# A two-layer graph network on one core: loop relations loaded two groups ahead, a last block read with 128 partitions, a ring of 30 gathered rows

## The chip, the cores and the metric

The kernel runs on one core of one Trainium2 chip. The metric is the time on the device in microseconds (us). Traces come from one profiled execution; times of kernels come from several.

## The reference

Two layers of a relational graph network over 50,000 nodes of 128 numbers and 850,000 edges (source, destination, one of 16 relations), sorted by destination. Every node has an edge to itself, a "loop", among them. All is float32.

```python
def layer(h, src, dst, rel, basis, w_comp, loop_w, bias):
    W = einsum('rb,bio->rio', w_comp, basis)          # 16 relations from 8 bases
    agg = segment_sum(h[src], dst * 16 + rel)         # per node and relation
    return relu(einsum('nri,rio->no', agg, W) + h @ loop_w + bias)

h = layer(x, ...); h = layer(h, ...)
out = layernorm(x + h)
```

## The kernel before

The 800,000 edges that are not loops are packed into 12,500 *tiles* of 128 edges; ten tiles make a *chunk* `c` (625 in a layer), five a half chunk. For each tile a gather (`gather`, L184, an indirect DMA that POOL issues) fetches the 128 source rows into a place `g` of a ring; a matmul (L1112, in `pa`) multiplies the place by the one-hot weights `hot`, ACT copies the result to `aT` (L1126). Every four chunks are multiplied by the bases (L796), turned (L805), spread over the nodes' slots on DVE (L779) and added to the nodes' sums with matmuls of L840. The ring has `RING * PER` = 5 x 5 = 25 places; after the last matmul of a half chunk `fetch` issues the gathers of the five tiles that stand 25 further. So a gather waits for the matmul that last read its place. The first 25 gathers of a layer go out at once.

Of every 45 or 50 tiles one is not gathered by POOL: SP or ACT copies its 128 rows one by one (`row_by_row`, L1022), finishing four half chunks (`LEAD`) ahead of their use, into places outside the ring.

Nodes are handled in *groups* `g` of 512 (98 in a layer; group 97 is smaller). `own_of_all` makes each group's loop part beside the chunks, two steps a chunk. `from_itself` loads `h_own`, the rows of four groups (L710, on SP, 128 partitions of 8 KB; 53 partitions for groups 96 and 97), at the first of each four; `loop_weights` then loads `lrel`, the loops' relations of the same four groups (L670, also on SP, 8 rows of 2 KB), and a step later small matmuls (L681, in `po<-twos,lrel`) and DVE (L689, L633, L662) make weights of it. Two more steps on, the transposes of `h_own` (L726) and the matmuls of L746 follow. At a layer's end the last sums are made by L768.

The edges are sorted out while layer 1 runs, by `later_rows`: `runs` closes up 128 runs of 672 edges a time and writes the others to `FULL` (L389) and the loops' relations to `LREL` (L444), both by indirect DMAs of POOL (scatters). `rows_of(j)` reads a block of closed-up runs back from `FULL` (L458, on SP, in two parts, of 1,280 numbers a partition), and DVE adds the parts (L465). The blocks start at rows 0, 16, 120, 248 and so on; the eleventh and last starts at 1,144 and has 106 rows. `own_of_all` takes care that the runs which a load of `lrel` needs have been stored, and notes up to where `LREL` has been read (`loaded`).

The order of the work on each engine is the order in which the code is written out: each engine runs its instructions in that order.

Of the kernel before, what the change touches and what calls it, by code (L numbers as in the profile page):

```python
# [39 lines left out]
F32 = mybir.dt.float32  # L40
# [10 lines left out]
P = 128  # L51
# [5 lines left out]
RUN = 672  # L57
HALF = K // 2
LIVE = HALF * P
# [8 lines left out]
BANK = 512  # L68
WEIGHTS = AT * PER * 8
BITS_AT_ONCE = BANK - WEIGHTS  # L70
RING = 5
SPANS = (9, 10)
LEAD = 4
HELD = 3
# [4 lines left out]
NEAR = 128  # L79
# [11 lines left out]
def tile_rgcn_resnorm(  # L91
# [16 lines left out]
    N, D = x.shape  # L108
    NR, NB = w_comp1.shape
    E = edges.shape[1] // 3  # L110
    R, M = -(-E // RUN), E - N
    C = -(-M // (K * P))
    NG = -(-R // P)
    GN, NGR = J * P, -(-N // (J * P))
    T = P // NR // 2

    ROWS = list(range(0, 2 * C, P)) if 2 * C <= P else [0, FIRST, *range(P - 8, 2 * C, P)]
    NP = NG * P * LIVE
# [14 lines left out]
    FULL = dram.tile([2 * NP, 2], F32, name="FULL")  # L133
# [62 lines left out]
    def column(j, first, ap):  # L196
# [3 lines left out]

    rows = [consts.tile([P, D], F32, name=f"g{i}") for i in range(RING * PER)]
    came_of = [tc.alloc_semaphore(f"row{i}") for i in range(RING * PER)]
    filled_times = [0] * (RING * PER)
    src = consts.tile([P, 2 * C * HALF], U16, name="src")

    APART = ((nc.sync, mybir.EngineType.SP), (nc.scalar, mybir.EngineType.Activation))
    apart = [
        [consts.tile([P, D], F32, name=f"g{RING * PER + HELD * i + j}") for j in range(HELD)] for i in range(len(APART))
    ]
# [47 lines left out]
    def set_up(pool):  # L257

        for h in range(2):
            nc.gpsimd.iota(  # L260
                spread[h],
                pattern=[[1, S]],
                base=-h * HALF * WN,
                channel_multiplier=-WN,
                allow_small_or_imprecise_dtypes=True,
            )
            ahead = pool.tile([HALF, S], F32, name="ahead")
            nc.vector.tensor_scalar(ahead, spread[h], 0.0, None, op0=OP.is_ge)
            nc.vector.scalar_tensor_tensor(spread[h], spread[h], float(WN), ahead, op0=OP.is_lt, op1=OP.mult)
        nc.gpsimd.iota(twos, pattern=[[2, T]], base=0, channel_multiplier=-1, allow_small_or_imprecise_dtypes=True)  # L270
        fits = pool.tile([2 * T, T], F32, name="fits")
        nc.vector.tensor_scalar(fits, twos, 0.0, None, op0=OP.is_le)
        nc.vector.scalar_tensor_tensor(twos, twos, -1.0, fits, op0=OP.is_ge, op1=OP.mult)
        later = pool.tile([HALF, 1], F32, name="later")
        nc.vector.tensor_scalar(later, part[:HALF], float(HALF), None, op0=OP.add)
        po = ps_o.tile([P, BANK], F32, name="po")
        nc.tensor.matmul(po[:S, :1], spread[0], part[:HALF], start=True, stop=False)
        nc.tensor.matmul(po[:S, :1], spread[1], later, start=False, stop=True)
        nc.vector.scalar_tensor_tensor(within[:S], po[:S, :1], float(-WN), part[:S], op0=OP.mult, op1=OP.add)
        yield  # L280
        none = pool.tile([P, NL // P], F32, name="none")
        nc.vector.memset(none, 0.0)
        for h in range(2):
            nc.sync.dma_start(LREL[h * NL : (h + 1) * NL].rearrange("(p k) o -> p (k o)", p=P), none)
        yield
# [166 lines left out]
    def rows_of(j, pool):  # L452

        r0 = ROWS[j]
        m = (ROWS[j + 1] if j + 1 < len(ROWS) else 2 * C) - r0
        parts = [pool.tile([P, LIVE, 2], F32, name=name) for name in ("full", "parts")]
        for h in range(2):
            nc.sync.dma_start(  # L458
                parts[h][:m],
                FULL[h * NP + r0 * LIVE : h * NP + (r0 + m) * LIVE].rearrange("(p e) w -> p e w", e=LIVE),  # L460
            )
        if j:
            yield
# [142 lines left out]
    def chunked():  # L606
        with (
# [5 lines left out]
            def ks(c):  # L613
                return min(K, -(-M // P) - c * K)
# [6 lines left out]
            def first(g):  # L621
                return max(0, -(-(g * GN - NEAR) // (N // C)) - 1)
# [7 lines left out]
            def summed_over(kinds, k):  # L630

                terms = hp.tile([P, K, NB, NR], F32, name="terms", bufs=1)[:, :k]
                nc.vector.tensor_tensor(  # L633
                    terms,
                    kinds[:, :, None, :].to_broadcast([P, k, NB, NR]),
                    table[:, None, :, :].to_broadcast([P, k, NB, NR]),
                    op=OP.mult,
                )
                return terms
# [23 lines left out]
                    weighed_for[i] = to  # L663
                    yield

            def loop_weights(g, n):

                few = min(T, NGR - g)
                of_nodes = hp.tile([2 * T, GN], F32, name="lrel", bufs=1)
                nc.sync.dma_start(  # L670
                    of_nodes[: 2 * few],
                    bass.AP(
                        tensor=LREL.tensor,
                        offset=LREL.offset + g * GN,
                        ap=[[GN, few], [NL, 2], [1, GN]],
                    ),
                )
                yield
                which_rel = ps_o.tile([P, BANK], F32, name="po")[:, : few * J]
                for j in range(J):  # L680
                    nc.tensor.matmul(  # L681
                        which_rel.rearrange("p (t j) -> p j t", j=J)[:, j],
                        of_nodes[: 2 * few].rearrange("q (p j) -> q j p", j=J)[:, j],
                        twos[: 2 * few, :few],
                        start=True,
                        stop=True,
                    )
                both = hp.tile([P, T * J, NR], U8, name="both_kinds", bufs=1)
                nc.vector.tensor_tensor(  # L689
                    both[:, : few * J],  # L690
                    col[:, None, 1 : NR + 1].to_broadcast([P, few * J, NR]),
                    which_rel[:, :, None].to_broadcast([P, few * J, NR]),
                    op=OP.is_equal,
                )
                yield
                lw = hp.tile([P, T * J, NB], F32, name="lw")
                for k in range(0, few * J, K):
                    m = min(K, few * J - k)
                    terms = summed_over(both[:, k : k + m], m)
                    nc.vector.tensor_reduce(lw[:, k : k + m], terms, AX.X, OP.add)  # L700
                yield lw.rearrange("p (t j) b -> p j t b", t=T)
# [175 lines left out]
                for _ in steps:  # L877
                    pass

            loaded, stored = [0], [1]  # L880
            rest_of_set_up = set_up(pr)
            next(rest_of_set_up)
            first_runs = runs(0, pr, lambda: 0)
# [16 lines left out]
            def later_rows():  # L900
                g = 0
                for j in range(1, len(ROWS)):
                    while g < needed(j):
                        g += 1
                        yield from runs(g, pr, lambda: loaded[0])
                        stored[0] = g + 1
                    yield from rows_of(j, pr)
                    ready[0] = j
                while g < NG - 1:
                    g += 1  # L910
                    yield from runs(g, pr, lambda: loaded[0])
                    stored[0] = g + 1

            coming = later_rows()
            ordered = ExitStack()
            ordered.enter_context(tc.manual_schedule(engines={mybir.EngineType.PE, mybir.EngineType.Pool, mybir.EngineType.DVE, mybir.EngineType.Activation, mybir.EngineType.SP}))
            for n, of in enumerate((x, H1)):
# [31 lines left out]
                def own_of_all():  # L949

                    for g in range(NGR):
                        while now[0] < min(first(g) + LAG - 5, C - LAG - 2):
                            yield
                        if n == 0 and g % T == 0:
                            end = min(N, (g + T) * GN)
                            while stored[0] < min(NG, -(-(end + NEAR) * E // (N * RUN * P))):
                                next(coming)
                            loaded[0] = end
                        yield from from_itself(g, of, n)
                        made[0] = g + 1  # L960

                def add(c):

                    for g in to_nodes(c, n):
                        assert made[0] > g
                        ending.append(finish(g, n))
# [65 lines left out]
                def place_in_ring(t):  # L1032

                    turn, k = divmod(n * tiles + t, RING * PER)
                    return k if turn % 2 == 0 else k // PER * PER + PER - 1 - k % PER
# [39 lines left out]
                for c in range(C):  # L1075
# [6 lines left out]
                    if c == 0:  # L1082
                        fetch(range(RING * PER))
                        nc.vector.tensor_copy(table, COMP[n].rearrange("p r b -> p b r"))
# [18 lines left out]
                    for k in range(0, K, PER):  # L1103
                        m = min(PER, ks(c) - k)
# [47 lines left out]
    def summed():  # L1152
        L1 = dram.tile([N, D], F32, name="L1")
        L2 = dram.tile([N, D], F32, name="L2")
        with tc.tile_pool(name="io", bufs=2) as io, tc.tile_pool(name="sbf", bufs=2) as sb:
# [140 lines left out]
            nodes(L2, norm, also=x)  # L1296

    chunked()
    wrong = nc.values_load(bad[0:1, 0:1], min_val=0, max_val=1)
    with tc.If(wrong > 0):  # L1300
# [40 lines left out]
```

## Time and profile before

| | us |
|---|---|
| median of 3 runs (lowest, highest) | 15,246.5 (15,244.9, 15,247.5) |
| profiled execution, its own time | 15,244.2 |
| its span, first to last instruction | 15,242.5 |
| busy: PE, DVE, ACT, POOL | 11,634.5, 10,276.1, 2,167.7, 11,380.2 |
| first gather starts, first gather of layer 2 starts, end | 30.3, 7,665.0, 15,242.5 |

The granted clock of PE was 0.811 on average. In rows of the timeline, the first number is the start in us, the second how long it took; in brackets stands how long the engine had been idle, and what ended that. In rows of groups, "busy, mean ns | idle before" follow the count. "issue" is idle time in which nothing that the profile shows was waited for.

### The profile page before, as it was taken

Reading aid. Unit: us, or ns where it says so; the run is one execution under the profiler, and the core shown is the slowest. Engines: PE = TensorE matmul, PEld = TensorE weight load, DVE = VectorE, ACT = ScalarE, POOL = GpSimd, SP = SyncE. Lnnn points to the kernel's source line nnn. Section 1 sums busy time; section 2 is a strip of 40 time slices with the busy share of each in tenths; the row PEclk is TensorE's granted clock in tenths of the full one; section 3 lists DMA queues with packets and bytes.
Section 4 is the critical chain, followed back from the end, with each engine's and each line's share of the span. In section 5 each row is a group of like instructions: output and inputs, shape, how many; then the busy total and the mean of one; then the engine's idle time right before and its main releaser. Section 6 shows DMA issues by size and latency. Waiting matters only on the chain.

```text
span 15242.5 us, 256609 instructions
## 1 busy us (share of the span) xinstructions
PE 11634.5 (76%) x43954; PEld 7253.0 (48%) x43954; DVE 10276.1 (67%) x11737; ACT 2167.7 (14%) x4309; POOL 11380.2 (75%) x12013
## 2 busy tenths in 40 slices
PE   6777777777777777777777877777777777777777
PEld 4444444444444444444444444444444444444444
DVE  8777777777666666666666666666666666666666
ACT  1111111111111111111111111111111111111111
POOL 6777777777777777777777777777777777777776
PEclk8788888878888888888878888888788888878888
DMA  2333333323222222222222223222232223222322
GB/s 80 75 74 73 70 75 73 70 69 72 66 62 62 62 65 62 62 62 65 57 63 66 66 65 68 65 66 65 64 68 65 65 64 68 65 66 65 68 65 57
DMA packets 584455, 1013.83 MB, mean 67 GB/s; under 512 B 265788, under 2 KB 335420, under 8 KB 576543
## 3 DMA queue, kind: packets, MB, share of 16 engines
q0 software_dynamic: 385232, 792.77, 23.4%
q1 hardware_dynamic: 131496, 186.50, 4.4%
q10 hardware_dynamic: 66064, 18.03, 1.0%
q14 instruction: 1308, 10.71, 0.2%
q8 instruction: 355, 5.82, 0.2%
HBM read 924.65 MB, written 71.59 MB: 65 GB/s over the span
## 4 chain that ended last, share of the span: by engine, by line
POOL 15%; PE 15%; DMA 14%; issue 8%; ACTq 7%; SPq 4%; DVE 4%; ACT 1%; DVEq 0%; POOLq 0%
POOL g L184 15%; DMA g<-H,at 7%; PE po L796 6%; ACTq L1022 5%; DMA g<-in_x_dram,at 4%; SPq L1022 3%; PE pn L840 3%; PE pa L1112 3%; DMA lrel<-LREL 3%; ACTq L1015 2%; PE po L746 2%; DVE ls L761 1%; SPq L1015 1%; DVE terms L633 1%; DVE by L753 0%
## 5 line engine op out<-in xcount | busy, mean ns | idle before, releaser
L184 POOL DMA_INDIRECT g<-in_x_dram,at x5990 | 5689.7, 950 | 1907.9 <-issue 1701.5
L184 POOL DMA_INDIRECT g<-H,at x5990 | 5665.9, 946 | 1901.6 <-issue 1707.5
L1112 PEld LDWEIGHTS pa<-hot,g 128*128 128x128 f32 x25000 | 4250.8, 226 | 4305.6 <-issue 1628.6
L1112 PE MATMUL pa<-hot,g 128*128 128x96 f32 x25000 | 4799.7, 319 | 1914.1 <-DMA g<-H,at 953.0
L840 PE MATMUL pn<-slots,own 120*128 120x512 f32 x4128 | 2765.0, 797 | 701.0 <-DVE own L819 347.7
L753 DVE TENSOR_TENSOR by<-po,lw 128x512 f32<-128x512 f32 x1568 | 1074.2, 685 | 3207.3 <-PE po L746 3203.7
L1126 ACT COPY aT<-pa 128x480 f32<-128x480 f32 x2500 | 1395.5, 558 | 8454.8 <-PE pa L1112 3866.2
L796 PE MATMUL po<-aT,basis 128*128 128x480 f32 x4960 | 2335.8, 629 | 74.9 <-ACT aT L1126 74.5
L746 PE MATMUL po<-basis,hT 128*128 128x512 f32 x3136 | 1994.4, 723 | 387.3 <-ACT hT L732 320.4
L662 DVE TENSOR_REDUCE fixed<-terms 128x80 f32<-128x1280 f32 x1250 | 1864.1, 1491 | 30.4
L633 DVE TENSOR_TENSOR terms<-kinds,fixed 128x1280 f32<-128x1280 uint8 x1250 | 1848.6, 1479 | 12.2
L761 DVE TENSOR_REDUCE ls<-by 128x128 f32<-128x1152 f32 (+1 forms) x784 | 1659.1, 2116 | 33.7 <-DVE by L753 0.4
L796 PEld LDWEIGHTS po<-aT,basis 128*128 128x128 f32 x4960 | 1040.7, 216 | 1169.8 <-issue 1086.8
L840 PEld LDWEIGHTS pn<-slots,own 120*128 120x128 f32 x4128 | 898.8, 246 | 1340.2 <-issue 584.7
L929 DVE TENSOR_TENSOR hot<-fixed,own 128x960 f32<-128x960 f32 x1250 | 1438.7, 1151 | 40.5 <-PE pa L1112 18.6
L779 DVE TENSOR_TENSOR slots<-po,which 120x1024 f32<-120x1024 f32 (+1 forms) x630 | 759.9, 1206 | 197.0 <-PE po L805 167.3
L746 PEld LDWEIGHTS po<-basis,hT 128*128 128x128 f32 x3136 | 564.2, 225 | 424.7 <-ACT hT L732 346.7
L689 DVE TENSOR_TENSOR both_kinds<-col,po 128x256 uint8<-128x256 f32 (+1 forms) x50 | 20.8, 416 | 793.4 <-PE po L681 793.4
L819 DVE TENSOR_SCALAR own<-col,node 120x256 f32<-120x256 f32 (+1 forms) x1250 | 425.1, 341 | 7.5 <-PE pn L840 7.5
L800 ACT COPY by_slot<-po 128x480 f32<-128x480 f32 x310 | 173.3, 559 | 1778.2 <-PE po L796 1636.8
L681 PE MATMUL po<-twos,lrel 8*128 8x4 f32 (+1 forms) x400 | 100.4, 370 | 413.4 <-DMA lrel<-LREL 413.4
L1049 ACT CAST at<-src 128x20 int32<-128x20 uint16 x626 | 129.7, 207 | 1929.0 <-issue 1922.7
(143 smaller groups left out, 3957.3 us busy)
## 6 DMA issues: line engine op xcount, KB each, us to landing
g<-in_x_dram SPq DMA_DIRECT2D x17536, 0.5 KB
g<-H SPq DMA_DIRECT2D x17536, 0.5 KB
g<-in_x_dram ACTq DMA_DIRECT2D x15744, 0.5 KB
g<-H ACTq DMA_DIRECT2D x15744, 0.5 KB
g<-in_x_dram,at POOLq DMA_INDIRECT x5990
g<-H,at POOLq DMA_INDIRECT x5990
H<-ls SPq DMA_DIRECT2D x97, 256.0 KB
xw<-in_x_dram SPq DMA_DIRECT2D x97, 256.0 KB
```

The source lines that it names most:

```text
L184: return nc.gpsimd.indirect_dma_start(out=to, out_offset=None, in_=of, in_offset=bass.IndirectOffsetOnAxis(ap=idx, axis=0))
L633: nc.vector.tensor_tensor(terms, kinds[:, :, None, :].to_broadcast([P, k, NB, NR]), table[:, None, :, :].to_broadcast([P, k, NB, NR]), op= ...
L662: nc.vector.tensor_reduce(to[:, : ks(i)], terms, AX.X, OP.add)
L746: nc.tensor.matmul(hb[:m], hT[:, j, :m], BASIS[n][:, b : b + few, :].rearrange("p b d -> p (b d)"), start=True, stop=True,)
L753: nc.vector.tensor_tensor(by[:m, b : b + few, :], hb[:m].rearrange("p (b d) -> p b d", d=D), lw[:m, j, g % T, b : b + few, None].to_broadc ...
L761: nc.vector.tensor_reduce(ls[:m, j, :], by[:m].rearrange("p b d -> p d b"), AX.X, OP.add)
L796: nc.tensor.matmul(ps[:, : BATCH * S], BASIS[n][:, b, :], aT[:, b, :], start=b == 0, stop=b == NB - 1)
L840: nc.tensor.matmul(sums[g], own, of[:k].rearrange("s j d -> s (j d)"), start=c == first(g), stop=c == final(g),)
L929: nc.vector.tensor_tensor(hot[:, : ks(c)], pm[:, : ks(c), :, None].to_broadcast([P, ks(c), NB, WN]), own[:, : ks(c), None, :].to_broadcast ...
L1022: row = by.dma_start(to[e : e + 1, :].bitcast(U8), flat[ds(places[e % LOADED], 4 * D)].rearrange("(o d) -> o d", o=1),)
L1112: product = nc.tensor.matmul(pa[:, i * NB * WN : (i + 1) * NB * WN], row, hot[:, k + i].rearrange("e b w -> e (b w)"), start=True, stop=Tr ...
L1126: nc.scalar.copy(aT[:, :, place_of + k * WN : place_of + (k + m) * WN].rearrange("d b (i w) -> d i b w", w=WN), pa[:, : m * NB * WN].rearr ...
```

## The change

Three things: `RING` is 6, so the ring has 30 places and a half chunk's gathers stand 30 tiles ahead. `lrel` is loaded by a function of its own, `ask_loops`, called for the next four groups when the third of the present four begins, and for the second layer when the first has no group left. The last block of closed-up runs is read with 128 partitions, of which 106 are used.

```diff
-RING = 5
+RING = 6
...
+        read = P if j == len(ROWS) - 1 and r0 + P <= NG * P else m
         for h in range(2):
             nc.sync.dma_start(
-                parts[h][:m],
-                FULL[h * NP + r0 * LIVE : h * NP + (r0 + m) * LIVE].rearrange("(p e) w -> p e w", e=LIVE),
+                parts[h][:read],
+                FULL[h * NP + r0 * LIVE : h * NP + (r0 + read) * LIVE].rearrange("(p e) w -> p e w", e=LIVE),
             )
...
-            def loop_weights(g, n):
+            def ask_loops(g, n):
 
-                few = min(T, NGR - g)
-                of_nodes = hp.tile([2 * T, GN], F32, name="lrel", bufs=1)
+                end, few = min(N, (g + T) * GN), min(T, NGR - g)
+                if n == 0:
+                    while stored[0] < min(NG, -(-(end + NEAR) * E // (N * RUN * P))):
+                        next(coming)
+                    loaded[0] = end
+                asked[0] = hp.tile([2 * T, GN], F32, name="lrel", bufs=1)
                 nc.sync.dma_start(
-                    of_nodes[: 2 * few],
+                    asked[0][: 2 * few],
...
+            def loop_weights(g, n):
+
+                few = min(T, NGR - g)
+                of_nodes = asked[0]
                 yield
...
-                        if n == 0 and g % T == 0:
-                            end = min(N, (g + T) * GN)
-                            while stored[0] < min(NG, -(-(end + NEAR) * E // (N * RUN * P))):
-                                next(coming)
-                            loaded[0] = end
+                        if g == n == 0:
+                            ask_loops(g, n)
+                        elif g % T == T // 2 and g + T // 2 < NGR:
+                            ask_loops(g + T // 2, n)
                         yield from from_itself(g, of, n)
                         made[0] = g + 1
+                    if n == 0:
+                        ask_loops(0, 1)
```

Line numbers of the changed kernel are 1 to 11 higher. PE and DVE run the same instructions in the same order as before.

On POOL, at the start of layer 1, stand the gathers of the first tiles. The names g_86 to g_115 are the places of the ring; the next round begins with g_90, g_89 and so on. Before, from the 25th gather:

```order
L184 DMA g_110<-in_x_dram,at 128x128
L184 DMA g_90<-in_x_dram,at 128x128
L184 DMA g_89<-in_x_dram,at 128x128
L184 DMA g_88<-in_x_dram,at 128x128
L184 DMA g_87<-in_x_dram,at 128x128
L184 DMA g_86<-in_x_dram,at 128x128
L444 DMA LREL<-l_rel,l_to 100352x1
```

And now, from the same gather:

```order
L184 DMA g_110<-in_x_dram,at 128x128
L184 DMA g_111<-in_x_dram,at 128x128
L184 DMA g_112<-in_x_dram,at 128x128
L184 DMA g_113<-in_x_dram,at 128x128
L184 DMA g_114<-in_x_dram,at 128x128
L184 DMA g_115<-in_x_dram,at 128x128
L184 DMA g_90<-in_x_dram,at 128x128
L184 DMA g_89<-in_x_dram,at 128x128
L184 DMA g_88<-in_x_dram,at 128x128
L184 DMA g_87<-in_x_dram,at 128x128
L184 DMA g_86<-in_x_dram,at 128x128
L444 DMA LREL<-l_rel,l_to 100352x1
```

Five gathers have come in ahead of the first one that needs a place freed, and the scatter to LREL stands five gathers later.

On SP, near the end of layer 1, the loads for groups 96 and 97 stand among the copies of single rows (g_112, TENSOR_LOAD fetches their addresses). Before:

```order
L1015 TENSOR_LOAD far
L1022 DMA g_112<-in_x_dram 1x512 x8
L710 DMA h_own<-in_x_dram 53x2048
L670 DMA lrel<-LREL 4x1x512
L1022 DMA g_112<-in_x_dram 1x512 x24
```

Now the load of lrel, and 28 rows of the order later that of h_own:

```order
L1033 DMA g_117<-in_x_dram 1x512 x18
L675 DMA lrel<-LREL 4x1x512
L1033 DMA g_117<-in_x_dram 1x512 x14
L1026 TENSOR_LOAD far
L1033 DMA g_118<-in_x_dram 1x512 x32
```

```order
L1033 DMA g_117<-in_x_dram 1x512 x32
L1026 TENSOR_LOAD far
L1033 DMA g_117<-in_x_dram 1x512 x8
L720 DMA h_own<-in_x_dram 53x2048
L1033 DMA g_117<-in_x_dram 1x512 x24
```

lrel has moved ahead of the copies of several tiles; h_own stands where it stood, with nothing of lrel behind it.

More of the change, by code (lines that the diff above doesn't have):

```diff
@@ L878, in done @@
                     pass
-            loaded, stored = [0], [1]
+            loaded, stored, asked = [0], [1], [None]
             rest_of_set_up = set_up(pr)
```

## The prediction

> **What bounds the kernel now.** I read the page's engine line first, then its groups, then POOL in the timeline and in the waits by stretch. No engine is busy the whole time, and the chain of waits spreads over many lines, so neither names the bound. The two gather groups on POOL do.
>
> ```profile
> PE 11634.5 (76%) x43954; PEld 7253.0 (48%) x43954; DVE 10276.1 (67%) x11737; ACT 2167.7 (14%) x4309; POOL 11380.2 (75%) x12013
> POOL 15%; PE 15%; DMA 14%; issue 8%; ACTq 7%; SPq 4%; DVE 4%; ACT 1%; DVEq 0%; POOLq 0%
> L184 POOL DMA_INDIRECT g<-in_x_dram,at x5990 | 5689.7, 950 | 1907.9 <-issue 1701.5
> L184 POOL DMA_INDIRECT g<-H,at x5990 | 5665.9, 946 | 1901.6 <-issue 1707.5
> ...
> 3003.32 0.95 POOL L184 DMA_INDIRECT g<-in_x_dram,at  x1 [0.30 <-issue]
> 3004.57 0.94 POOL L184 DMA_INDIRECT g<-in_x_dram,at  x1 [0.31 <-issue]
> ```
>
> A gather takes 0.948 us (11,355.6 over 11,980) and the next starts 0.30 us after its end, waiting for nothing that is shown: one gather per 1.253 us. In 11,980 gathers that pace alone is 15,010 us of the 15,242.5, so POOL is the bound although the page calls it 75% busy. Whatever shortens another engine's wait helps only where POOL itself stood still. The idle time before gathers is 3,809.5 us; 11,980 gaps of 0.305 make 3,654, so 156 us are real stops. The waits of POOL in ten consecutive stretches say where. The rows are, in order, from 0:125 (two), 125:3900, 3900:4000, 4000:7500, 7500:7570, 7570:7660, 7660:7700, 7700:15060, 15060:15130 and 15130:15243; columns are total us, times, longest.
>
> ```profile
> POOL g L184 <- PE pa L1112: 9.5, 1, 9.5
> POOL g L184 <- ACT at L1049: 8.5, 1, 8.5
> POOL g L184 <- PE pa L1112: 53.0, 126, 5.4
> POOL g L184 <- PE pa L1112: 14.7, 4, 13.8
> POOL g L184 <- PE pa L1112: 43.6, 131, 3.2
> POOL g L184 <- PE pa L1112: 17.0, 3, 16.3
> POOL g L184 <- PE pa L1112: 13.4, 4, 6.1
> POOL g L184 <- DMA lrel<-LREL: 16.0, 1, 16.0
> POOL g L184 <- PE pa L1112: 107.1, 277, 5.3
> POOL g L184 <- PE pa L1112: 16.9, 2, 16.6
> POOL g L184 <- PE pa L1112: 14.4, 6, 8.3
> ```
>
> Less 0.305 for each time these are 9.2, 8.2, 14.6, 13.5, 3.6, 16.1, 12.2, 15.7, 22.6, 16.3 and 12.6 us. "PE pa L1112" means that the ring is full: the place that POOL wants is freed by a matmul of L1112, and PE was late. The 8.2 (first numbers of rows) and the 15.7 (the second layer gathers from H, which has to be complete) are not touched by the change.
>
> **Relations of loops.** Here is one group of four in the middle: the two loads on SP, the matmul that reads lrel, POOL's stop behind it, and the transposes that read h_own.
>
> ```profile
> 13838.09 0.37 SPq L710 DMA_DIRECT2D h_own<-H  x1
> 13838.50 0.68 SPq L670 DMA_DIRECT2D lrel<-LREL  x1
> 13854.84 2.02 PE L681 MATMUL po<-twos,lrel 8*128 8x4 f32 x8 [12.93 <-DMA lrel<-LREL]
> 13860.58 0.94 POOL L184 DMA_INDIRECT g<-H,at  x1 [5.72 <-issue]
> 13869.98 0.68 PE L726 MATMUL po<-ident,h_own 32*128 32x32 f32 x8
> ...
> PE po L681 <- DMA lrel<-LREL: 413.4, 48, 27.0
> ```
>
> lrel is 16 KB but queued behind 1 MB of h_own and lands 16 us after its issue; PE stands 12.9 us, ring slack takes about 7 of that, and POOL stops for 5.4 beyond its usual gap (named "issue", but the same event). In the stretches outside the layers' ends these stops are 14.6 + 3.6 + 22.6 + 5.4 = 46.2 us. With lrel asked for two groups (about 155 us) earlier the matmul waits for nothing. What is late next is h_own: it landed before lrel, so within 16.8 us of its issue; the transposes would come 12.93 us sooner, 18.96 us after it. Where PE gets there earlier it waits a few us, and less than 7 cost POOL nothing even with 25 places, less than 13 with 30. Ends: 35, if for a quarter of these stops h_own is as late as lrel was, and 46; I take 45, because the row above leaves 2 us to spare and the ring more.
>
> **128 partitions.** The eleventh block of closed-up runs is read with 106 partitions, the tenth with 128. First the last block (two loads on SP, DVE's add, PE's wait), then the tenth.
>
> ```profile
> 3924.31 0.32 SPq L458 DMA_DIRECT2D parts<-FULL  x1
> 3963.76 0.83 DVE L465 TENSOR_TENSOR both<-full,parts 106x640 f32<-106x640 f32 x1 [18.55 <-DMA parts<-FULL]
> 3966.51 3.78 PE L840 MATMUL pn<-slots,own 120*128 120x512 f32 x4 [22.34 <-DVE slots L779]
> ...
> 3828.71 0.46 SPq L458 DMA_DIRECT2D parts<-FULL  x1
> 3843.96 0.81 DVE L465 TENSOR_TENSOR both<-full,parts 128x640 f32<-128x640 f32 x1
> ```
>
> 106 partitions took 39.5 us from issue to use, 128 at most 15.3, without a wait. The 24 us are more than DVE's 18.55, so the wait goes, PE's 22.34 with it, and POOL's 13.5. Reading 22 unused partitions twice is 225 KB on a queue that had room. What a denser load can do to gathers on their way is seen once, shortly after an earlier block of 128 partitions:
>
> ```profile
> 2088.13 0.74 PE L1112 MATMUL pa<-hot,g 128*128 128x96 f32 x2 [5.45 <-DMA g<-in_x_dram,at]
> ```
>
> PE waited 5.45 us for a gather; POOL had no stop of that kind there. Ends 8, if those 5.45 us came back on POOL, and 13.5, which I take, since a gather that lands late is not issued late.
>
> A rule of the Trainium skill speaks against this part: "DMA: Bandwidth & Descriptors", section "Queues, rings and completion order", says that each DMA engine takes turns between its queues at packet granularity, draining a whole packet of one before it switches, so that a load spread over all engines stands ahead of gathers on all of them. If that counted, this term would be the lower end and the sum 81; if the row counts, it stays. The trace agrees with the rule as to PE's wait, and not as to POOL.
>
> **The ends of the layers.** The last group of four has two groups; h_own has 53 partitions there. The rows are its loads, the matmul, POOL's stop, the transposes, and the DMA queue of SP from 7509 to 7528.
>
> ```profile
> 7500.15 0.23 SPq L710 DMA_DIRECT2D h_own<-in_x_dram  x1
> 7529.78 1.99 PE L681 MATMUL po<-twos,lrel 4*128 4x2 f32 x8 [26.17 <-DMA lrel<-LREL]
> 7535.18 0.95 POOL L184 DMA_INDIRECT g<-in_x_dram,at  x1 [16.35 <-PE pa L1112]
> 7538.90 0.68 PE L726 MATMUL po<-ident,h_own 32*128 32x32 f32 x8
> q1 hardware_dynamic: 48, 0.39, 5.3%
> ...
> 15097.40 2.00 PE L681 MATMUL po<-twos,lrel 4*128 4x2 f32 x8 [26.98 <-DMA lrel<-LREL]
> 15106.39 0.68 PE L726 MATMUL po<-ident,h_own 32*128 32x32 f32 x8
> ```
>
> 5.3% of sixteen engines is not quite one engine's time: h_own itself crawls over one, and the change leaves it at 53. lrel no longer waits behind it, but the transposes do, until about 7529.8. So PE gains only what it had to do between the matmul and the transposes: 9.1 us, and 9.0 in layer 2. POOL's stops of 16.1 + 12.2 and 16.3 + 12.6 shrink by more, but do not set the end, because PE is behind from here on:
>
> ```profile
> 7538.90:7655.90 117.00, 96.46 (x433) 62.55 (x432) 81.86 (x88) 15.99 (x30) 74.43 (x79) 0.90 0.21 51
> 15106.30:15226.80 120.50, 97.12 (x434) 64.24 (x432) 86.97 (x114) 18.52 (x38) 73.87 (x78) 0.87 0.22 53
> ```
>
> (From the transposes to the last gathered matmul: length, then busy PE, PEld, DVE, ACT, POOL, the granted clock, DMA.) Against POOL's 74 us, PE has 96 and DVE 82 to 87, and they feed each other. DVE's head start (it makes the loop weights during the wait) is worth some of PE's 20 idle us; I take 2. Gain 11 at each end, 22 together; ends 18 and 57, where 57 is all of POOL's stops.
>
> **The ring.** Five more gathers go out before the first stop: 5 x 1.253 = 6.3 of the 9.2 us. The first LREL scatter stands behind them on POOL; DVE's data for it are then ready, and that is within the 6.3. Later the ring adds 6.3 us of slack to each stop already counted above. The cast of row numbers moves on ACT by half a chunk; POOL needs it ten gathers later, 12.5 us, so nothing. Ends 0 and 9.2.
>
> **Sum.** 6.3 + 45 + 13.5 + 22 = 86.8. The profiled execution took 15,244.2, so 15,157; the median of the runs is 2.3 above it, so 15,160.
>
> **Rivals.** (a) The ends are paced by POOL after all: 57 in place of 22, 15,125. For it: PE and DVE both have idle time there. Against: no matmul of L1112 waits for a gather between 7538.9 and 7655.9, though POOL stopped. (b) h_own takes lrel's place as the late load in the middle too, half of 45 stays and the ends give 18: 15,186. For it: h_own is the 1 MB, and lrel only followed. Against: the 19 us above. (c) Slower: lrel in layer 1 must follow the LREL scatter on POOL, which runs up to a ring, 30 x 1.253 = 37.6 us, behind SP's place in the program. SP is in order and would hold its row copies:
>
> ```profile
> 2999.94 27.81 SPq L1022 DMA_DIRECT2D g<-in_x_dram  x70
> ```
>
> At 0.397 us, 128 copies need 51 of the 54 us in which they are due, so SP regains little. The copies are four half chunks (25 us) ahead, so a hold costs PE up to 12.6 us; at 24 loads, 302: 15,462. It decides from 3.6 us a load. Against: in the order, one load of the 24 stands within ten tiles behind its scatter. (d) It does nothing, because PE's other waits fill the ring as often: 15,246. Against: each stop in the middle follows an lrel wait or the one block.
>
> **How the numbers follow.** The forecast, 15,140 to 15,175, has 0.70; (a) 0.10; (b) 0.11; (d) 0.05; (c) 0.04. From (a) to a little above (b), 15,122 to 15,200, leaves out about 0.13 and holds the bounds of the terms. A measurement here tells 0.2%, 30 us, from no change. Faster takes the first three, 0.90; the same 0.06; slower 0.04.
>
> **What would show it.** Right: PE's wait for lrel gone; at L726 a wait for h_own near 17 us, twice, and otherwise under 3; DVE's wait for the last block under 3 us; POOL's stops for PE under 15 us outside the start and the last 150 us of a layer; gathers still at 0.95 + 0.30. Wrong: a longer gather or gap, which at 0.007 us each would eat the gain; waits of PE for copied rows; a layer end that moves by over 15 us or under 5.

## The result: 33 us faster, not 87, and the profile after

The changed kernel takes 15,211.5 us (median of 17 runs, 15,206.7 to 15,216.9) against 15,244.5 of the kernel before (17 runs, 15,238.7 to 15,248.2): a ratio of 0.9979, 95% interval 0.9972 to 0.9985. The forecast was 15,160, its range began at 15,122 and ended at 15,200.

The page of the changed kernel, its engine line, chain and gather groups:

```profile
PE 11727.4 (77%) x43954; PEld 7319.2 (48%) x43954; DVE 10281.8 (68%) x11737; ACT 2146.8 (14%) x4309; POOL 11359.3 (75%) x12013
SPq 6%; PE 3%; ACTq 3%; issue 2%; DMA 2%; POOL 1%; DVE 1%; ACT 0%; DVEq 0%; POOLq 0%
L184 POOL DMA_INDIRECT g<-in_x_dram,at x5990 | 5678.2, 948 | 1891.0 <-issue 1696.8
L184 POOL DMA_INDIRECT g<-H,at x5990 | 5655.7, 944 | 1902.6 <-issue 1725.2
```

From first to last gather, layer 1 became 29.9 us shorter and layer 2 15.5. The stretch from the last gather of layer 1 to the first of layer 2 grew from 16.6 to 22.9 us, the one after the very last gather from 25.9 to 32.4. Together this is 32.6 of the span's 32.7 us (15,242.5 to 15,209.8). In this trace a gather is on average 1.8 ns shorter than in that of before; that comes and goes between executions and is not the change (below).

POOL's waits in the changed kernel, by stretch. The rows are from 0:125 (two), 125:3900, 3900:4000, 4000:7480, 7480:7550, 7550:7630 (two), 7630:7650, 7650:15030, 15030:15100 and 15100:15210; columns are total us, times, longest:

```profile
POOL g L184 <- ACT at L1060: 8.5, 1, 8.5
POOL g L184 <- ACT aT L1137: 6.2, 1, 6.2
POOL g L184 <- PE pa L1123: 43.5, 121, 4.6
POOL g L184 <- PE pa L1123: 0.6, 2, 0.3
POOL g L184 <- PE pa L1123: 64.8, 154, 7.2
POOL g L184 <- PE pa L1123: 12.4, 3, 10.5
POOL g L184 <- ACT aT L1137: 6.7, 1, 6.7
POOL g L184 <- PE pa L1123: 6.0, 4, 4.6
POOL g L184 <- issue: 23.8, 6, 22.3
POOL g L184 <- PE pa L1123: 112.8, 266, 7.5
POOL g L184 <- PE pa L1123: 5.3, 4, 4.0
POOL g L184 <- PE pa L1123: 15.7, 4, 8.3
```

Less 0.305 us a time, the start fell from 9.2 to 5.9 and the 13.5 us of the last block are gone. But the three long stretches hold 6.6 + 17.8 + 31.7 = 56.1 us of stops, where there were 46.2. What 45 us of the forecast were to remove is still there. PE's waits say what for; first those of the whole span (total us, times, longest), then one group of four in the middle and the last groups of layer 1:

```profile
PE pa L1123 <- DMA g<-H,at: 889.9, 1229, 2.8
PE pa L1123 <- DMA g<-in_x_dram,at: 828.8, 1111, 4.8
...
PE po L736 <- DMA h_own<-H: 169.8, 15, 19.8
PE po L736 <- DMA h_own<-in_x_dram: 141.6, 16, 27.3
...
PE pa L1123 <- DMA g<-H: 41.7, 11, 8.2
```

```profile
4405.19 0.37 SPq L720 DMA_DIRECT2D h_own<-in_x_dram  x1
4419.80 1.03 PE L736 MATMUL po<-ident,h_own 32*128 32x32 f32 x8 [9.99 <-DMA h_own<-in_x_dram]
...
7480.22 2.02 PE L691 MATMUL po<-twos,lrel 4*128 4x2 f32 x8
7483.61 0.24 SPq L720 DMA_DIRECT2D h_own<-in_x_dram  x1
7517.23 1.03 PE L736 MATMUL po<-ident,h_own 32*128 32x32 f32 x8 [27.32 <-DMA h_own<-in_x_dram]
```

The wait for lrel is gone, and 31 waits for h_own, 311 us in all, stand in its place. The last row of the waits is new too: PE waits for rows that were copied one by one, which it never did before.

### The profile page after: what moved, and what is told of

Same layout as the page of the kernel before. It is cut to its first block, busy times and chain, and to the rows that moved or that the text cites. A ratio compares the mean times of both kernels' runs of the same rounds, so it can differ in the third digit from the quotient of the medians.

```text
span 15209.8 us, 256696 instructions
## 1 busy us (share of the span) xinstructions
PE 11727.4 (77%) x43954; PEld 7319.2 (48%) x43954; DVE 10281.8 (68%) x11737; ACT 2146.8 (14%) x4309; POOL 11359.3 (75%) x12013
## 5 line engine op out<-in xcount | busy, mean ns | idle before, releaser
L850 PE MATMUL pn<-slots,own 120*128 120x512 f32 x4128 | 2811.4, 809 | 669.1 <-DVE own L829 340.2
L806 PE MATMUL po<-aT,basis 128*128 128x480 f32 x4960 | 2359.6, 635 | 105.8 <-ACT aT L1137 105.5
L756 PE MATMUL po<-basis,hT 128*128 128x512 f32 x3136 | 1993.2, 722 | 398.7 <-ACT hT L742 335.7
L634 DVE TENSOR_TENSOR terms<-kinds,fixed 128x1280 f32<-128x1280 uint8 x1250 | 1848.7, 1479 | 12.2
L806 PEld LDWEIGHTS po<-aT,basis 128*128 128x128 f32 x4960 | 1052.2, 219 | 1215.3 <-issue 1098.3
L736 PE MATMUL po<-ident,h_own 32*128 32x32 f32 x3136 | 335.1, 256 | 311.5 <-DMA h_own<-H 169.8
L736 PEld LDWEIGHTS po<-ident,h_own 32*128 32x128 f32 x3136 | 288.5, 173 | 363.2 <-issue 230.9
```

The lines of the kernel that those rows point to most:

```text
L634: nc.vector.tensor_tensor(terms, kinds[:, :, None, :].to_broadcast([P, k, NB, NR]), table[:, None, :, :].to_broadcast([P, k, NB, NR]), op= ...
L756: nc.tensor.matmul(hb[:m], hT[:, j, :m], BASIS[n][:, b : b + few, :].rearrange("p b d -> p (b d)"), start=True, stop=True,)
L806: nc.tensor.matmul(ps[:, : BATCH * S], BASIS[n][:, b, :], aT[:, b, :], start=b == 0, stop=b == NB - 1)
L850: nc.tensor.matmul(sums[g], own, of[:k].rearrange("s j d -> s (j d)"), start=c == first(g), stop=c == final(g),)
```

## What is slow: by all signs one DMA engine

Two theories were set against each other. **Q**: without lrel's wait PE runs ahead of SP, whose queue is nearly full, so h_own is issued too late. **E**: the DMA engine that carries the single rows is too slow, and whatever has a part on it lands late.

E comes from the time between issue and landing (the arrival of the data). The page gives it for the ten scatters to FULL and to LREL (last number, median us); first before, then after:

```profile
FULL<-full,to_i POOLq DMA_INDIRECT x10, 10.6
LREL<-l_rel,l_to POOLq DMA_INDIRECT x10, 7.8
```

```profile
FULL<-full,to_i POOLq DMA_INDIRECT x10, 13.5
LREL<-l_rel,l_to POOLq DMA_INDIRECT x10, 12.6
```

A gather has no such row, but where PE waits for one, the time from its end on POOL to PE's start is its landing time. For SP's copies, the n-th packet of their size on SP's DMA queue belongs to the n-th copy. In layer 2, medians in us at 0 to 500, 2,000 to 2,500, 4,000 to 5,000 and 6,000 to 7,000 us after the layer's first gather:

| kernel | copied tiles, both layers | gather: end on POOL to landing | SP's copy: issue to start of its packet |
|---|---|---|---|
| before | 520 | 2.1, 10.8, 10.9, 11.3 | 1.0, 8.5, 7.9, 8.7 |
| changed | 520 | 2.4, 11.2, 13.7, 13.4 | 1.0, 9.3, 11.0, 11.1 |
| e4_span | 496 | 2.3, 2.8, 3.3, 2.9 | 0.9, 1.0, 1.1, 1.0 |
| e14_span10 | 492 | 2.3, 3.6, 3.5, 3.5 | 1.0, 1.2, 1.2, 1.2 |
| e8_alt | 508 | 2.2, 4.4, 3.6, 4.1 | 1.0, 1.7, 1.2, 1.7 |
| e12_514_48 | 514 | 2.5, 4.4, 4.7, 4.1 | 1.0, 2.0, 2.3, 1.6 |
| e13_532 | 532 | 2.4, 14.8, 14.8, 14.3 | 1.2, 12.1, 12.0, 12.2 |
| e15_half | 520, half rows | 2.0, 8.4, 12.9, 14.7 | 1.0, 6.2, 10.4, 12.0 |

The front part's 12,500 tiles are those of both layers, 6,250 each; of every 45 SP copies one, and of every 50 ACT, 520 in all.

With 520 copied tiles layer 2 begins with everything landing at once and then falls behind, some 9 us in 2,000, or 0.4%, an estimate from the table. It goes on until the ring is full and POOL has to stop, and each stop lets the DMA catch up a little: the plateau is at 11 us before, 12 with the larger ring alone, 13 with lrel early alone, 13.5 in the changed kernel. From there on the ring holds POOL to the pace of the DMA, and that is what the small stops in the middle are. That pace is no fixed figure. From 4,200 to 7,000 us into layers 1 and 2 the gathers start on average 1.253 and 1.258 us apart in the kernel before, 1.257 and 1.262 in the changed one, and 1.249 in both layers of e4_span, where nothing is late. Why the changed kernel's pace is the slowest of these is not shown; without its waits for h_own (e3_own, below) it is 1.253 and 1.259.

That a single engine is behind is inferred, since the records don't name engines. In the trace before, 69,376 packets of 512 B come from the queues of SP and ACT (66,560 of them copied rows), yet only 4.5% begin over 10 ns before the end of the one ahead; of the gathers' 191,687 packets of 4 KB (16 a gather), 93% do. The two queues keep out of each other's way: an ACT packet of 512 B begins inside one of SP in 0.9% of cases, and the other way round in 0.1%; with one queue's times shifted by 1 us it would be 11% and 9%. So the rows of both queues go through one thing, one at a time. The Trainium skill, "DMA: Bandwidth & Descriptors", section "Why a DMA increments its semaphore by 16 and not by 1", says that a DMA of SP or ACT uses the largest number of engines, up to 16, that divides the slowest dimension of more than one element on both of its sides, and takes the lowest-numbered ones. By that a load of 53 partitions is on one engine. For a single row the trace decides: each copy is one packet, not several, and one engine, if it is the lowest-numbered one, is the same for both queues. The trace agrees as far as it can: packets in single file.

## The experiments

Each ratio is to the kernel before, timed beside that run. The median of the kernel before lay between 15,244.5 and 15,252.8 us from one such set to the next, so a difference of two runs from different sets is uncertain by up to 8 us.

**The three edits alone**, each on the kernel before.

```diff
-RING = 5
+RING = 6
```

> The kernel before with the ring of 30 places alone. Two theories of why the changed kernel gained 33 us and not 87. Q (the queue of SP): with lrel early, PE runs ahead of SP, SP issues h_own too late, and h_own takes lrel's place. E (one DMA engine): all copies of single rows of SP and ACT go over one of the 16 DMA engines, every gather has a sixteenth of its rows there, and that engine cannot keep up with POOL; in the traces of before and after the gathers land 1.5 us after their issue at a layer's start and 11.5 (ring 25) or 14 us (ring 30) after it from about 3,000 us on. Q expects that the ring alone absorbs most of the middle's stops of at most 5.4 us, each under 6.3: 15,185 to 15,200. E expects that the five places fill up with gathers that wait for that engine (landing about 14 us after issue in the later part of each layer) and that little is left: 15,225 to 15,240, of which 6 at the start.

Measured 15,241.2; ratio 0.9995 (0.9986 to 1.0004), 7 us that can't be told from nothing. Gathers landed after 12 us late in the layer, 11 before: the places filled with rows on their way. Q's 15,185 to 15,200 is out; E's range is missed by 1 us.

```diff
-                of_nodes = hp.tile([2 * T, GN], F32, name="lrel", bufs=1)
+                of_nodes = asked[0]
```

(with `ask_loops` and its calls as in the change)

> The kernel before with lrel asked for two groups ahead, and nothing else (ring 25, last block with 106 partitions). Q: PE waits for h_own instead, as in the changed kernel, 10 to 20 us a time in the later parts of the layers, and the stops stay as they were but for the ends: 15,220 to 15,235. E: the same wait, because h_own too lands 14 us late through that one engine, and the gathers' landing stays at 11 to 12 us in the plateau, limited by the ring; 15,220 to 15,235. It shares out the 33 us, and does not tell Q from E.

15,231.6; 0.9989 (0.9980 to 0.9998): 17 us, inside the range of both theories, which it was not made to part.

```diff
-                parts[h][:m],
+                parts[h][:read],
```

> The kernel before with the last block read with 128 partitions alone. The forecast's term: POOL's stop of 13.5 us near 3,970 us goes, 15,231 to 15,237. Rival, from E: that stop was also time in which the one engine caught up, and it is given back within the layer: 15,240 to 15,246. It also shows if gathers last 946 ns (median) as in the kernel before or 944 as in the changed one.

15,241.0; 0.9993 (0.9984 to 1.0002): 9 us against the kernel before in those runs (15,249.9), under the forecast's 13.5 and not told from nothing. As a time it lies in the rival's range, as a gain between the two, so it does not decide. Its gathers last 948 and 944 ns, as in the changed kernel, though it has neither of the other edits: the 1.8 ns are no effect of the change. The three gains add up to 33, as much as the whole change gave, but two of them are not told from nothing, so the sum proves little.

**h_own earlier**, on the changed kernel.

```diff
                 for j in range(J):
+                    if j == 1 and g % T == T - 1 and g + 1 < NGR:
+                        ask_own(g + 1, of)
```

(`ask_own` is the load of L720, taken out of `from_itself`)

> The changed kernel with h_own of the next four groups asked for while the last group of the present four is at its second matmul of L756, some 40 us earlier in SP's program; nothing else. PE's waits for h_own go in either theory. Q: they were what filled the ring, so the middle gains its 45 us and the ends some 20: 15,145 to 15,165. E: the engine sets the pace in the later part of each layer, the gathers land 14 us or more after their issue as before and POOL goes on stopping for the ring; the ends gain, the middle gains under 15: 15,180 to 15,200.

15,200.6; 0.9969 (0.9957 to 0.9981): 11 us less than the changed kernel, where Q had 45 to 65. No wait for h_own is left; PE's waits for rows show where they went:

```profile
PE pa L1129 <- DMA g<-in_x_dram,at: 650.1, 874, 5.5
PE pa L1129 <- DMA g<-H,at: 597.5, 823, 4.2
PE pa L1129 <- DMA g<-H: 471.2, 62, 26.2
...
PE pa L1129 <- DMA g<-in_x_dram: 365.0, 50, 23.2
```

836 us of waits for copied rows, 67 in the changed kernel. The kernel found another late transfer.

**Fewer copied tiles**, on the changed kernel; POOL gathers the tiles that are no longer copied.

```diff
-SPANS = (9, 10)
+SPANS = (9, 11)
```

> The changed kernel with ACT's copied tiles 11 half chunks apart, not 10: 496 copied tiles for 520, SP's copies as before, 24 more gathers on POOL (24 x 1.253 = 30 us). Q: SP's queue is unchanged, h_own is as late as in the changed kernel, the stops stay and 30 us are added: 15,235 to 15,245. E: the one engine has 4.6% fewer copies, so gathers land under 6 us after issue to the end of a layer, h_own lands within 9 us of its issue, and POOL's stops in the middle fall under 15 us: 15,211 + 30 - 70 = 15,160 to 15,185.

15,136.0; 0.9926 (0.9913 to 0.9940): 75 us faster than the changed kernel, with 24 more gathers. First the scatters' landing, then all waits for h_own, then POOL's for the ring:

```profile
FULL<-full,to_i POOLq DMA_INDIRECT x10, 6.2
LREL<-l_rel,l_to POOLq DMA_INDIRECT x10, 3.6
```

```profile
PE po L736 <- DMA h_own<-in_x_dram: 8.5, 2, 7.0
PE po L736 <- DMA h_own<-H: 2.2, 1, 2.2
```

```profile
POOL g L184 <- PE pa L1123: 138.0, 452, 0.3
```

452 ordinary gaps of 0.3 us and not one stop. The last packet of h_own's 1 MB, at the same place in SP's order, now ends 4 to 6 us after its issue; in the later part of the changed kernel's layers it took 13 to 18. A tile that is not copied is gathered, so the bytes stay as they were (1,013.6 MB, 1,014.1 in the changed kernel): a limit on all bytes together does not explain this. E's range was missed by 24 us; the stops at the ends went as well.

A third theory was left, that ACT's own queue had been relieved. So ACT keeps its copies, and SP has fewer:

```diff
-SPANS = (9, 10)
+SPANS = (10, 10)
```

> The changed kernel with SP's copied tiles 10 half chunks apart, not 9: 492 copied tiles, ACT's 246 as they were, 28 more gathers (35 us). E: it makes no difference whose copies are fewer; gathers land about 3 us after issue, copies of both queues about 1 us after theirs, POOL has no stops in the middle: 15,136 + 4 x 1.253 = 15,141, give or take 5. A third theory, A: with 496 it was ACT's own queue that was relieved (its copies of results to aT came sooner), not a DMA engine; then PE's waits for ACT stay at their 441 us, ring and stops stay, and 28 gathers come on top: 15,235 to 15,250.

15,171.2; 0.9949 (0.9935 to 0.9963), 25 us above E's upper bound; the profiled execution, the shortest of five, took 15,153.7. A's 15,235 is out, as the landing and POOL's waits for the ring show:

```profile
POOL g L184 <- PE pa L1123: 135.6, 427, 5.6
```

The one stop, 5.6 us, is at the end of layer 2. PE still waits for ACT's results of L742 as long as in the changed kernel (314.5 us against 335.7; 152.6 in e4_span), though its wait for aT at L806 fell from 105.5 to 22.6. So a lighter queue of ACT may be worth some of what lies between this run and e4_span, 18 us between the profiled executions and 35 between the medians, of which four more gathers are 5; that part was not tested by itself.

The kernel before, with 496 copied tiles:

```diff
-SPANS = (9, 10)
+SPANS = (9, 11)
```

> The kernel before (ring 25, lrel late, 106 partitions) with 496 copied tiles instead of 520, and nothing of the change. E: the engine keeps up, so lrel lands about 5 us after its issue although it still stands behind h_own, PE's waits for it fall from 12.9 to a few us and the stops in the middle go; what the three edits are then worth is 3 to 6 at the start, up to 13.5 at the last block and a few us at the ends: 15,136 + 4 to 24 = 15,140 to 15,160. The forecast's own theory, by which lrel behind 1 MB is what fills the ring: the waits and stops stay, and 24 gathers come on top: 15,245 + 30 = 15,275.

15,139.7; 0.9925 (0.9911 to 0.9939). This is e4_span without any of the three edits; the 4 us between them are less than the two sets of runs differ by. lrel still stands behind 1 MB in the queue:

```profile
PE po L681 <- DMA lrel<-LREL: 61.3, 16, 18.3
```

48 waits of 413 us have become 16 of 61. Being second in the queue was not what made lrel late. Once that engine keeps up, the change has next to nothing left to gain.

On the changed kernel again, with every other step of ACT's a half chunk longer:

```diff
-            for q in range(20 + span * i // len(SPANS), 2 * C - LEAD, span):
+            at = 20 + span * i // len(SPANS)
+            while at < 2 * C - LEAD:
...
+                at += span + (i * len(of)) % 2
```

> The changed kernel with ACT's copied tiles 10 and 11 half chunks apart in turn: 508 copied tiles, half way between 520 and 496, and 12 gathers fewer than with 496. E, if 2.3% fewer copies are enough for the engine to keep up (its gathers came 12 us later over some 3,000 us of a layer, 0.4%): landing under 8 us, no stops in the middle, 15,136 - 15 = 15,121. E, if the engine has no room at 508: landing climbs to 14 us late in the layers, 15,140 to 15,180. Q: 15,225, the changed kernel's time and 12 gathers.

15,125.6; 0.9919 (0.9905 to 0.9932), 5 us above E's estimate for an engine that keeps up. 508 tiles are few enough.

**More copies, and lighter ones**, on the changed kernel. First every other step of ACT's a half chunk shorter (the rest of the edit as in e8_alt):

```diff
+                at += span - (i * len(of)) % 2
```

> The changed kernel with 532 copied tiles instead of 520: ACT's 9 and 10 half chunks apart in turn, 12 gathers fewer on POOL. By POOL's pace: 15,211 - 15 = 15,196. E: the engine is the slower one, so more copies make the kernel slower although POOL issues less; by at least as much as 12 tiles fewer made it faster in the saturated part (0.4% of some 10,000 us): 15,235 to 15,300, landing limited by the ring at about 14 us, POOL's stops over 100 us in the middle.

15,498.7; 1.0160 (1.0146 to 1.0174). Slower with fewer gathers, as E says, but far beyond its bound. The landing is at 14.8 us, and PE also waits for ACT, which had the new copies to issue:

```profile
PE po L759 <- ACT hT L745: 844.9, 182, 12.8
PE po L809 <- ACT aT L1140: 632.8, 189, 7.6
```

These waits are 336 and 106 us in the changed kernel. This run has at least two causes and does not price the engine.

```diff
-                                    to[e : e + 1, :].bitcast(U8),
-                                    flat[ds(places[e % LOADED], 4 * D)].rearrange("(o d) -> o d", o=1),
+                                    to[e : e + 1, : D // 2].bitcast(U8),
+                                    flat[ds(places[e % LOADED], 2 * D)].rearrange("(o d) -> o d", o=1),
```

(and the places of copied rows are set to zero once, at the start; the second half of every copied row is left out, so the output is not that of the reference)

> The changed kernel with 520 copied tiles, where each single copy moves the first 256 B of its row and leaves out the second half (which stays zero); as many copies on SP and ACT, and as many gathers, as in the changed kernel. E, if the engine's time goes by bytes: it keeps up, gathers land about 3 to 5 us after issue, 15,136 - 30 = 15,106 (15,095 to 15,115). E, if it goes by pieces: as the changed kernel, 15,205 to 15,217, landing 14 us. A: the queues of SP and ACT are as before, 15,205 to 15,217.

15,183.5; 0.9958 (0.9944 to 0.9971): 28 us faster, a quarter of what E by bytes expected, and its landing climbs more slowly to the same height. It fits neither of E's two prices, by bytes or by pieces, and A does not explain a gain with both queues as they were. If half a row costs nothing extra of its own, which was not tested, the 256 B are the smaller part of a copy's price there.

```diff
-                                    to[e : e + 1, :].bitcast(U8),
+                                    to[e : e + 1, :].bitcast(U8).rearrange("p (k d) -> p k d", k=2),
```

(and the same of the source)

> The changed kernel, its 520 copied tiles kept, with every row copied as two pieces of 256 B instead of one of 512 B, so that each copy is spread over two DMA engines. E, if that engine's time goes by bytes: it keeps up, gathers land within about 4 us to a layer's end, POOL's stops in the middle go, as with 496 copied tiles, but without the 24 more gathers: 15,136 - 30 = 15,106. E, if its time goes by pieces (each copy still puts one piece and one semaphore write on it): gathers still land 14 us after issue and the time stays, 15,200 to 15,220. Q: SP's queue has the same number of copies; if each takes longer than the 0.397 us of now SP falls behind its 54 us, and PE waits for copied rows: over 15,250.

Inconclusive. 15,214.8; 0.9979 (0.9969 to 0.9988). The trace still has 35,072 packets of 512 B on SP's queue: the two pieces were merged into one again, so this is a second run of the changed kernel.

**The ends**, on the changed kernel, then with 508 and 514 copied tiles.

```diff
+                    rows = (end - g * GN) // (A * J)
+                    most = rows // 16 * 16
+                    for r0, r1 in ((0, most), (most, rows)):
...
```

> The changed kernel with the last h_own load of each layer in two parts, of 48 partitions and of 5, instead of one of 53; nothing else. E: the 53 rows of 8 KB all go over the one engine that already has the copies of single rows (33 us); 48 take three rows on each of sixteen, so h_own lands about 15 us after its issue, as for the other groups, PE's waits of 27.3 and 19.7 us fall to under 14, and the ends gain 5 to 12 us each: 15,190 to 15,202. Rival: the ends are set by PE's own work after the last gather, and h_own is only the first of several waits there: 15,208 to 15,213.

15,186.3; 0.9958 (0.9944 to 0.9971): 25 us less than the changed kernel, 28.5 less than e5_cut2, which is the same kernel and was run in the same set; the expected range began at 15,190. At the end of layer 1, the two loads and the transposes:

```profile
7481.43 0.69 SPq L724 DMA_DIRECT2D h_own<-in_x_dram  x2
7494.42 0.65 PE L740 MATMUL po<-ident,h_own 32*128 32x32 f32 x8 [1.23 <-DMA h_own<-in_x_dram]
```

1.2 us for 27.3: the load of 53 rows took 33 us, 48 and 5 took 13.

> 508 copied tiles, and the last h_own load in parts of 48 and 5 partitions. E: with the engine keeping up the load of 53 made PE wait only some 2 us at each end, so the split is worth 0 to 5 us here, not the 25 that it gave with 520: 15,120 to 15,126. If the load of 53 costs by its own length whatever else the engine does: 15,100 to 15,110.

15,108.1; 0.9904 (0.9889 to 0.9919), the fastest of all and the version to keep: 144.7 us less than the kernel before in those runs. The two edits are those of e8_alt and e6_48. The split is worth some 17 us here, not 0 to 5: I had counted PE's short wait and not what 53 rows of 8 KB may hold up on that engine, where their last packet still ends 22 us after the issue with 496 or 508 tiles; that this is the reason is argued, not shown.

Then 514 tiles, against e11_508_48:

```diff
-                at += span + (i * len(of)) % 2
+                at += span + (i * len(of) % 4 == 1)
```

> 514 copied tiles, and the split last load. Gathers landed about 4 us after issue with 508 and 14 with 520. If the engine still keeps up at 514: six gathers fewer, 15,113 to 15,118. If not, the landing climbs within each layer and stops return in the middle: 15,125 to 15,170.

15,117.4; 0.9910 (0.9895 to 0.9925). No stop in the middle, so the engine keeps up, but only just: in layer 1, which the table leaves out, gathers land after 8.9 us between 4,000 and 5,000 us and after 4.4 later. It is slower than 508 by 9, with three gathers fewer a layer. In its trace the stretch between the layers is 22.7 us and the one at the end 30.8, against 13.3 and 24.1 with 508; why, I did not settle.

## Why the prediction was wrong, step by step

- **POOL as the bound (11,980 x 1.253 us).** This step failed first. It is the bound at the beginning of each layer, and throughout with 508 tiles or fewer; in the later part of the layers the transfers set the pace (1.258 us a gather in layer 2 where POOL's own step is 1.251), and POOL's stops are how it shows. I took each stop for a loss that its releaser caused, when most were due anyway: 24 copied tiles fewer, and no edit of the change, gave 15,139.7. The profile had it: scatters that land after 8 and 11 us, and lrel's 16.
- **The middle, 45 us.** The term that failed: 46.2 us of stops became 56.1, and the edit alone gave 17 us, ends included. That lrel is late because it is "queued behind 1 MB of h_own" was the wrong reading of a right row, as e10_before496 shows. That "the row above leaves 2 us to spare" took h_own's issue and PE's place as fixed to each other, 19 us apart; without lrel's wait PE came to the transposes mostly 0 to 14 us after the issue, and in the later part of the layers waited 4 to 20 us. Rival (b) named this wait and gave it 0.11; its 15,186 kept half of the 45 and 18 of the 22 at the ends, and neither was there.
- **The ends, 22 us.** POOL's stops there, two short ones for ACT counted in, shrank by 4 and 9 us, and the stretches without gathers behind them grew by 6.3 and 6.5: little is left. That growth is the ring's: e1_ring, with the ring alone, has 23.0 and 32.5 us there, e2_loops, with lrel early alone, 17.2 and 26.1. That the 53 rows crawl over one engine was seen, and that PE is behind from there on (from the transposes to the last gathered matmul it is 117.0 and 120.2 us, 117.0 and 120.5 before); but PE now wanted h_own 6.3 and 12.7 us after its issue, and waited 27.3 and 19.7 us for it, where it had waited 26.2 and 27.0 for lrel. e6_48 shows what could be had there: 25.
- **The last block, 13.5.** Right in place: POOL's stop is gone and DVE's wait fell from 18.55 to 3.23 us. Alone it gave 9, with an interval that reaches past nothing. In the trace of e7_read the stop is gone too, and yet POOL's idle time before gathers beyond 0.305 us a time is 170 us, where it was 156: stops came back elsewhere, while its gathers were 22 us shorter in sum. Whether gathers on their way paid for the denser load, the lower end's reason, this does not decide.
- **The ring, 6.3.** The start gained 3.3, since after the five gathers POOL waits 6.2 us for ACT. The whole edit alone measured 7. What goes out early at a layer's start also runs out early at its end, as the longer stretches there show.
- **The signs.** PE's wait for lrel went and gathers stayed at 0.95 + 0.30, as foretold. That there would be "a wait for h_own near 17 us, twice, and otherwise under 3" did not hold, DVE's wait for the last block is 3.23 where under 3 was said, and two signs of error came: PE's waits for copied rows, and layer ends that moved by under 5 us.
- **Rival (c)**, SP held by the scatter to LREL, did not decide anything: e2_loops, with that edit alone, is faster.

## What to carry to other kernels

Read how long transfers take from issue to landing, early and late in a long loop, before calling the issuing engine the bound: a time that grows until a ring is full and then stays means that the transfers set the pace, and then a removed wait comes back as another one. A mean over sixteen DMA engines can hide one that is full; look for transfers that cannot be spread, such as single rows or 53 partitions. Here 2.3% fewer single rows were worth 86 us, the three edits 33.

## What the runs showed of the hardware

- 520 x 128 single rows of 512 B beside 11,980 gathers in some 15,200 us are just too many, and late in the layers gathers then land 11 to 14 us after POOL's end; with 514 x 128 or fewer POOL has no stop in the middle. That the limit is one DMA engine's, with these rows and a sixteenth of each gather on it, is inferred. The page's line shows two to three tenths for the mean of sixteen. Adding up what this engine would carry in the trace before (all packets of 512 B of SP's and ACT's queues, the 4 B ones of these queues, a sixteenth of the rest) gives about 63%, an estimate; what fills the remainder is open.
- A gather on POOL takes 944 to 946 ns (mean in layer 2), alike through that layer and differing between executions. e11_508_48's profiled one has 946 and took 15,139.4 us, its three others 15,105.7 to 15,109.7; 11,992 gathers at 2.4 ns more are 29 us. The other three were not profiled, so that they have 944 is inferred. The profiled ones of e10_before496 and e12_514_48 are 29 and 32 us above their medians in the same way. The kernel before had 946 in its trace and no such difference, as it would where POOL does not set the pace.
